# x in two layouts, s_dst as a row sent by DMA, norms scaled on either engine, and issue by due time, in a four-layer graph kernel

## The chip, the cores and the metric

One core of one Trainium2 chip. The metric is the device time of one execution in microseconds (us). Every kernel here was timed in several rounds beside the kernel before on the same chip, and its result compared with the reference. A program can fall into a slower state. Where a kernel is named, "after" is the changed kernel.

## The reference, cut to what matters

64 graphs of 256 nodes with 128 features share one adjacency matrix. Four layers follow each other, each closed by a layer norm of (x + layer(x)) without weights. The kernel treats two graphs at a time (a "pair"; 32 pairs).

```python
# layer 0, five steps
    m_in = jnp.einsum('nm,bmd->bnd', in_matrix, h)         # av = [m_in, m_out]; both matrices are adj
    z = jax.nn.sigmoid(av @ w3_w.T + w3_b + u3)             # u3 = h @ u3_w.T + u3_b
    r = jax.nn.sigmoid(av @ w4_w.T + w4_b + u3)
    hv = jnp.tanh(av @ w5_w.T + w5_b + (r * h @ u5_w.T + u5_b))
    h = (1.0 - z) * h + z * hv
# layer 1: a product with fixed softmax weights (cut)
# layer 2, attention
    h = jnp.einsum('bmi,ih->bmh', x, Wp) + bp
    s_src = jnp.einsum('bmh,h->bm', h, a_src)
    s_dst = jnp.einsum('bmh,h->bm', h, a_dst)
    scores = s_src[:, :, None] + s_dst[:, None, :]          # leaky relu, mask, softmax, times A
    h_gat = jax.nn.relu(_layernorm(jnp.einsum('bmn,bnh->bmh', weighted_adj, h), gat_g, gat_b))
    # then an aggregation, two products with a norm between them, relu(... + h_gat) (cut)
# layer 3: polynomials of adj, each with its weight (cut)
x = _layernorm(x + layer(x))                                # after every layer
```

There are six norms per pair, 192 in all: four between layers, one after the attention, one inside layer 2.

## The kernel before: the parts that the change touches

The kernel describes its work as operations with tiles read and written, an engine and a duration. A small list scheduler of its own (`Schedule`) orders them, and they are then emitted to the tile framework in that order. The parts that matter:

```python
# Schedule.order: the next operation is the one with the least key
key = (start + (us if len(op.ways) > 1 else 0.0), min(op.pair, self.n_pairs - ABREAST), -op.rest, op.number)
...
# every norm: statistics on VectorE, the root on GpSimd
def stats(y, eps=None):
    ...
    pool(1.04, lambda: nc.gpsimd.tensor_tensor(rs(), rs(), neg_half.ap, op=ALU.pow), [s, neg_half], [s])   # L422
    return s, mv, rs
# five of six norms: scaled on VectorE, (x - mean) * rs, straight from the root
def layer_norm(y, o):
    s, mv, rs = stats(y)
    ... nc.vector.tensor_scalar(tokens(o)[:, c, :], tokens(y)[:, c, :], mv()[:, c, 0:1], rs()[:, c:c + 1],
                                op0=ALU.subtract, op1=ALU.mult)                                          # L430
def layer0(x0):
    hT = to_sbuf(transposes(x0, tokens), "hT")            # x turned by TensorE
    ...
def layer2(x2):
    ...
    # s_dst, already repeated on all partitions, by one product of 512 columns
    pe(mm(512), lambda: nc.tensor.matmul(sd.at(512), vdst.ap, xT.at(512), start=True, stop=True), [vdst, xT], [sd])
    ...
    # the attention norm only: -mean * rs on VectorE (L549), then four activations on ScalarE (L553)
# emission, at the end
for op, fn in S.order(tiles):
    for v, ap in op.tiles.items():
        v.ap = ap
    fn()
```

## Time and profile before

| | before |
|---|---|
| time, median of 3 | 1832.8 us (1831.24 to 1833.34) |
| TensorE (PE) busy | 1741.1 us, 95% |
| PE idle, 50 to 1600 us | 36 us |
| PE idle, from 1600 us on | 49 us |
| VectorE (DVE) / ScalarE (ACT) busy | 1194.5 / 793.5 us |
| GpSimd (POOL) busy | 438.8 us |

Read it as: an engine that is almost always busy, with a short tail where it is not. The idle times are lengths of a stretch less PE's busy time in it; the prediction shows the lines.

### The profile page before, as it was taken

Reading aid. Unit: us, or ns where it says so; the run is one execution under the profiler, and the core shown is the slowest. Engines: PE = TensorE matmul, PEld = TensorE weight load, DVE = VectorE, ACT = ScalarE, POOL = GpSimd, SP = SyncE. Lnnn points to the kernel's source line nnn. Section 1 sums busy time; section 2 is a strip of 40 time slices with the busy share of each in tenths; the row PEclk is TensorE's granted clock in tenths of the full one; section 3 lists DMA queues with packets and bytes.
Section 4 is the critical chain, followed back from the end, with each engine's and each line's share of the span. In section 5 each row is a group of like instructions: output and inputs, shape, how many; then the busy total and the mean of one; then the engine's idle time right before and its main releaser. Section 6 shows DMA issues by size and latency. Waiting matters only on the chain. (4 is left out here: it accounts for less than half of the span.)

```text
span 1832.3 us, 22228 instructions
## 1 busy us (share of the span) xinstructions
PE 1741.1 (95%) x7856; PEld 1230.3 (67%) x7856; DVE 1194.5 (65%) x3536; ACT 793.5 (43%) x1586; POOL 438.8 (24%) x519
## 2 busy tenths in 40 slices
PE   8999999999999999999999999999999999998767
PEld 6567576767767667676776666666766667665566
DVE  5466666667767667667776577665667666665753
ACT  3444445444445454434444444444444444443322
POOL 0022212312231221222222212231123222111152
PEclk9999999999999999999999999999999999999778
DMA  4000000000000000000000000000000000000000
GB/s 119 1 1 12 12 12 1 12 12 13 7 12 7 18 6 7 12 13 11 8 13 12 13 12 1 12 12 7 7 0 7 6 7 7 6 1 6 1 1 24
DMA packets 35024, 20.50 MB, mean 11 GB/s; under 512 B 1248, under 2 KB 34528, under 8 KB 34912
## 3 DMA queue, kind: packets, MB, share of 16 engines
q1 hardware_dynamic: 34912, 19.08, 3.6%
q8 instruction: 61, 1.00, 0.2%
q14 instruction: 51, 0.42, 0.1%
HBM read 10.69 MB, written 8.39 MB: 10 GB/s over the span
## 5 line engine op out<-in xcount | busy, mean ns | idle before, releaser
L173 ACT COPY a<-ps 128x512 f32<-128x512 f32 (+1 forms) x532 | 278.5, 541 | 483.5 <-PE ps L400 286.0
L419 POOL TENSOR_SCALAR s<-s 128x4 f32<-128x4 f32 x160 | 49.5, 310 | 986.1 <-DVE s L416 986.1
L400 PE MATMUL ps<-aT,a 128*128 128x256 f32 x1024 | 242.8, 379 | 1.7 <-ACT a L173 1.6
L400 PEld LDWEIGHTS ps<-aT,a 128*128 128x128 f32 x1024 | 189.9, 190 | 49.5 <-issue 24.5
L422 POOL TENSOR_TENSOR s<-s,neg_half 128x4 f32<-128x4 f32 x192 | 200.4, 1044 | 15.9
L430 DVE TENSOR_SCALAR x<-a,s 128x128 f32<-128x128 f32 x384 | 120.9, 370 | 100.1 <-POOL s L422 99.9
L462 DVE TENSOR_TENSOR a<-a,a 128x512 f32<-128x512 f32 x160 | 121.0, 756 | 95.4 <-ACT a L460 95.2
L460 ACT ACTIVATE a<-ps,bzrh 128x512 f32<-128x512 f32 x160 | 109.9, 687 | 160.6 <-PE ps L458 160.5
L446 ACT ACTIVATE a<-ps,bzrh 128x512 f32<-128x512 f32 x160 | 109.4, 685 | 160.1 <-PE ps L443 156.8
L448 DVE SCALAR_TENSOR_TENSOR a<-a,a 128x512 f32<-128x512 f32 x160 | 120.9, 759 | 81.1 <-ACT a L446 80.5
L414 DVE BATCH_NORM_STATS2 s<-a 128x6 f32<-128x128 f32 x640 | 141.5, 279 | 47.9 <-ACT a L173 45.7
L450 PE MATMUL ps<-a,w 128*128 128x512 f32 x320 | 163.0, 600 | 7.2 <-ACT a L446 7.0
L458 PE MATMUL ps<-a,u5h 128*128 128x512 f32 x320 | 164.4, 595 | 4.9 <-DVE a L448 4.9
L443 PE MATMUL ps<-a,w 128*128 128x512 f32 x320 | 163.6, 593 | 1.8 <-ACT a L173 1.8
L457 PE MATMUL ps<-a,w 128*128 128x512 f32 x320 | 164.5, 596 | 0.0
L442 PE MATMUL ps<-a,W 128*128 128x512 f32 x320 | 163.9, 594 | 0.0
L481 PEld LDWEIGHTS ps<-W,a 128*128 128x128 f32 x1024 | 131.7, 196 | 36.6 <-issue 17.9
L481 PE MATMUL ps<-W,a 128*128 128x128 f32 x1024 | 135.6, 281 | 8.7 <-DVE a L488 4.4
L452 ACT ACTIVATE a<-ps,bzrh 128x512 f32<-128x512 f32 x160 | 110.0, 688 | 62.7 <-PE ps L450 61.3
L400 PE MATMUL ps<-aT,x 128*128 128x256 f32 x512 | 129.3, 391 | 8.1 <-DVE x L430 7.7
L463 DVE SCALAR_TENSOR_TENSOR a<-a,a 128x512 f32<-128x512 f32 x160 | 118.5, 745 | 16.3 <-ACT a L452 13.9
L382 PEld LDWEIGHTS ps<-ident,a 128*128 128x128 f32 x768 | 92.4, 142 | 53.3 <-issue 23.2
(140 smaller groups left out, 2645.6 us busy)
## 6 DMA issues: line engine op xcount, KB each, us to landing
x<-x_in SPq DMA_DIRECT2D x32, 256.0 KB, 2.8
y_out<-a SPq DMA_DIRECT2D x32, 256.0 KB, 2.3
W<-mats_in SPq DMA_DIRECT2D x1, 832.0 KB, 6.7
W<-mats_in SPq DMA_DIRECT2D x1, 512.0 KB, 3.7
rbc<-rows_in SPq DMA_DIRECT2D x1, 385.0 KB, 7.2
aT<-adjT_in SPq DMA_DIRECT2D x1, 256.0 KB, 4.7
a<-adj_in SPq DMA_DIRECT2D x1, 256.0 KB, 5.9
ccol<-cols_in SPq DMA_DIRECT2D x1, 6.0 KB, 3.5
```

The source lines that it names most:

```text
L173: S.add([("ACT", us_act, lambda: nc.scalar.copy(o(), i())), ("DVE", us_dve, lambda: nc.vector.tensor_copy(o(), i()))], r, w)
L400: nc.tensor.matmul(t.at(2, N)[:, b, :], tokens(i)[:, 2 * b + j, :], right.ap[:, j, :], start=(j == 0), stop=(j == 1))
L414: nc.vector.bn_stats(st.at(4, 6)[:, c, :], tokens(y)[:, c, :])
L422: pool(1.04, lambda: nc.gpsimd.tensor_tensor(rs(), rs(), neg_half.ap, op=ALU.pow), [s, neg_half], [s])
L430: nc.vector.tensor_scalar(tokens(o)[:, c, :], tokens(y)[:, c, :], mv()[:, c, 0:1], rs()[:, c:c + 1], op0=ALU.subtract, op1=ALU.mult)
L442: nc.tensor.matmul(t.at(512), mat("u3"), hT.at(512), start=True, stop=False)
L443: nc.tensor.matmul(t.at(512), w345.ap[:, 1, :], mT.at(512), start=False, stop=True)
L450: pe(mm(512), lambda t=t, mT=mT: nc.tensor.matmul(t.at(512), w345.ap[:, 0, :], mT.at(512), start=False, stop=True, skip_group_check=True), ...
L457: nc.tensor.matmul(t.at(512), w345.ap[:, 2, :], mT.at(512), start=True, stop=False)
L458: nc.tensor.matmul(t.at(512), u5h.ap, r.at(512), start=False, stop=True)
L462: dve(0.7, lambda hv=hv, hT=hT: nc.vector.tensor_sub(hv.at(512), hv.at(512), hT.at(512)), [hv, hT], [hv])
L481: nc.tensor.matmul(tokens(t)[:, c, :], i.at(4, P)[:, c, :], w(), start=(k == 0), stop=(k == len(lefts) - 1))
```

## The change

Its intent: take work off TensorE (the first transposes of layer 0, because x is also loaded turned; the s_dst product, because s_dst comes as a column of a product that is made anyway, is turned on VectorE and goes over DRAM to all partitions), let the scheduler choose ScalarE or VectorE for the scaling of each norm, and order the operations so that the last pairs do not march in step. The core of the diff (set-up of weights, tuned durations and renamings cut):

```diff
-                    key = (start + (us if len(op.ways) > 1 else 0.0), min(op.pair, self.n_pairs - ABREAST), -op.rest, op.number)
+                    key = (start + (us if len(op.ways) > 1 else 0.0), self.due(op.pair) - op.rest, op.number)
...
+DUE, LAST_DUE, LAST = 50.0, 10.0, 7
+    def due(self, pair):
+        late = max(pair - (self.n_pairs - LAST), 0)
+        return DUE * (pair - late) + LAST_DUE * late
...
     def load_x(p):
+        load(lambda: hTs[p].at(2, N), xT[2 * p:2 * p + 2].rearrange("b d n -> d b n"), hTs[p])
...
-    def layer0(x0):
-        hT = to_sbuf(transposes(x0, tokens), "hT")
+    def layer0(x0, hT):
...
+        nmr = lambda: s.at(32)[:, 12:16]
+        dve(0.16, lambda: nc.vector.scalar_tensor_tensor(nmr(), mv()[:, :, 0], -1.0, rs(), op0=ALU.mult, op1=ALU.mult), [s], [s])
+        return s, rs, nmr
+
+    def normalize(y, o, s, rs, nmr):
+        ...
+        S.add([("ACT", 1.85, by_act), ("DVE", 1.45, by_dve)], [y, s], [o])
...
-        pe(mm(512), lambda: nc.tensor.matmul(sd.at(512), vdst.ap, xT.at(512), start=True, stop=True), [vdst, xT], [sd])
+        dve(0.34, lambda: nc.vector.transpose(srow.at(4, 32), hs()[:, :, D - 30:D + 2]), [h], [srow])
+        S.add([("SP", 0.45, lambda: nc.sync.dma_start(line([32, 4], [P, 4], [1, 32]), srow.at(4, 32)[31::32]))], [srow], [d], 3.2)
+        S.add([("SP", 0.45, lambda: nc.sync.dma_start(sd.at(512), line([0, P], [1, 512])))], [d], [sd], 5.5)
```

## The prediction

> **What bounds the kernel now.** I read four views of the profile, in this order. First the page's engine totals and its forty slices.
>
> ```profile
> span 1832.3 us, 22228 instructions
> ...
> PE 1741.1 (95%) x7856; PEld 1230.3 (67%) x7856; DVE 1194.5 (65%) x3536; ACT 793.5 (43%) x1586; POOL 438.8 (24%) x519
> ...
> PE   8999999999999999999999999999999999998767
> ...
> PEclk9999999999999999999999999999999999999778
> DMA  4000000000000000000000000000000000000000
> ```
>
> TensorE is busy 95% of the span, VectorE 65%, ScalarE 43%, the DMA engines almost never. The last three slices are different: TensorE falls to 0.7 to 0.8 busy, and its granted clock falls with it. So there are two regimes, and the second view, busy time by stretch (columns: stretch, length, busy time of PE, PEld, DVE, ACT, POOL, granted clock, DMA share, GB/s), measures them:
>
> ```profile
> 0.00:6.10 6.10, 0.00 (x0) 0.00 (x0) 1.99 (x14) 1.28 (x1) 0.83 (x7) 1.00 0.71 209
> ...
> 50.00:1650.00 1600.00, 1563.83 (x7047) 1094.49 (x7047) 1064.98 (x3082) 720.12 (x1427) 385.76 (x446) 1.00 0.03 9
> 1650.00:1832.30 182.30, 133.60 (x644) 106.31 (x642) 102.35 (x379) 56.17 (x130) 52.16 (x66) 0.84 0.03 8
> ```
>
> From 50 to 1650 us TensorE idles 36 us in 1600, at full clock. After 1650 it idles 49 us in 182 and runs at 0.84. The third view, the chain that ended last (start, length, what), shows why:
>
> ```profile
> 1656.41 6.91 PE ps L400 x32
> ...
> 1690.63 8.65 PE ps L400 x32
> ...
> 1757.60 1.22 POOL a L557
> 1758.82 1.23 POOL a L556
> ...
> 1789.96 10.18 PE ps L400 x32
> 1800.13 1.75 PE ps L382 x16
> ```
>
> One spread of one pair is 8 records (4 matmuls in two passes each), so x32 is four pairs doing the same stage one after the other: the last four pairs, which have equal priority, march in step. All four want TensorE together, then VectorE together, then GpSimd together. The same 32 records take 6.91 us at 1656 and 10.18 us at 1790: that is the lowered clock. The fourth view, groups by form, prices what the change removes:
>
> ```profile
> L382 PE MATMUL ps<-ident,x 128*128 128x128 f32 x512 | 77.5, 279 | 2.9 <-DVE x L430 2.9
> L505 PE MATMUL ps<-wpx,a 128*128 128x129 f32 x256 | 35.0, 277 | 0.0
> L510 PE MATMUL ps<-a,vdst 128*128 128x512 f32 x64 | 34.2, 616 | 0.0
> ```
>
> L382 on x is four sets of 4 transposes per pair, one of which goes; L510 is the s_dst product, which goes whole. The mean of one record overlaps its neighbours; the chain gives the true spacing: four transposes in 0.44 us, one 512-column product in 0.86 us, one spread in 1.73 us.
>
> **What the Trainium skill says.** (1) "TensorE: Matmul & The Clock Gate", Part 1: the clock is throttled unless the engine has been busy lately. The trace agrees: 1.00 where it idles 2%, 0.84 where it idles 27%. So an idle gap in the tail costs twice. (2) "Trace Analysis", Optimization Strategy: where the bound engine changes over time, interleaving the regimes may help. This tail is such a place: from 1700 to 1750 us DVE is busy 36.15 of 50 us and PE 35.67. (3) "VectorE: DVE Perf Modes", The three transpose paths: the VectorE transpose turns 32x32 blocks only. That is why s_dst comes out as four rows, one per block, and needs a DMA to be joined; no trace here has this operation yet. (4) "DMA: Bandwidth & Descriptors", Anatomy of one DMA: some 2.0 us fixed per transfer, and waits are taken by the issuing sequencer. The trace agrees: y_out lands 2.3 us after issue, x 2.8 us.
>
> **The change, part by part.** *x loaded in both layouts.* Removes the first transposes of layer 0: 32 x 0.44 = 14.1 us of TensorE, and 32 evacuations of 0.59 us, mostly on ScalarE. Adds 32 transfers of 256 KB, which are small beside a DMA share of 0.03. At the start, xT and x of pair 0 both stand ahead of adjT in the queue, so the first spread (6.9 us now) comes perhaps 0.8 us later; a product on xT can start ahead of it.
>
> *s_dst by block turn and DMA.* Removes 32 x 0.86 = 27.5 us of TensorE and one PSUM bank for that time. Adds one column to 128 products (35.0/129 = 0.3 us), 32 turns on DVE (estimate 0.3 us each, from the 128x128 forms at 0.28) and two DMAs in series: estimated 0.4 + 2.3 + 0.4 + 2.8 = 5.9 us against 0.86 us of product. This is in the chain of one pair but not of the core: the order keeps several pairs open at once, and the new schedule reserves more (0.45 + 3.2 + 0.45 + 5.5).
>
> *Norm scaling on ACT or DVE.* In the built order 101 of the 192 norms are on DVE and 91 on ACT (before: 160 and 32). The busy time of one scaling is (120.9 + 76.0)/640 = 0.31 us on DVE (the two L430 groups) and 49.5/128 = 0.39 us on ACT (L553). DVE loses 59 x 4 x 0.31 = 73 us and gains 160 x 0.16 = 26 us of the small -mean*rstd product and 10 us of turns: 1194 - 73 + 36 = 1157, give or take 30. ACT gains 59 x 4 x 0.39 = 92 and loses 24 copies of 0.59, 14: about 871 us, half of the span. Neither becomes the bound.
>
> *Issue by due time.* Moves nothing in amount, but the order changes throughout. I summed the TensorE work in the order in which the instructions stand, with the spacings above. Before, the last four pairs have 52, 51, 49 and 47 us of TensorE work left at their attention product, and 6.1, 4.3, 2.6 and 0.9 us at their last product: in step. After, the last seven have 133, 121, 109, 89, 86, 54 and 40 us left there, and 69.6, 55.7, 41.3, 28.2, 16.0, 8.2 and 0.9 at the end: a staircase, so while one pair normalizes another multiplies.
>
> **The sum, by stage.** The before kernel: the 639 records left at 1650 us are 112 us of work at the spacings above, and over the first 1650 us busy time was 1.5% above such a sum (1607.5 against 1584), so 113 us at full clock; they took 133.6 busy us. Slow clock thus cost 20 us. 1832 = 1721 (work) + 6 (start) + 36 (steady idle) + 49 (tail idle) + 20 (slow clock).
>
> After: work 1721 - 14.1 - 27.5 + 0.3 = 1679, since on an engine that is 98% busy removed work counts in full. Start 7. Steady idle 26: the waits there are short ones on DVE and ACT (longest 2.5 us), the planned durations are closer to the measured ones and a PSUM bank is freed; I take a quarter off. Tail idle: the last pair still has a chain after its attention product. Adding row durations (three norms at 1.75 + 1.3 + 0.2 + 1.5, GpSimd's 2.6, layer 2's and 3's products, copies, some 30 hops at 0.2, the last DMA) gives about 49 us, beside which 40 us of TensorE work stands; so at least 9 us, plus imperfect filling over the last 110 us, where those late layers ask about as much of DVE as of PE: 18. Slow clock 7, in proportion to that idle time. Sum: 1679 + 7 + 26 + 18 + 7 = 1737 us, 5.2% below.
>
> **Rivals.** *The staircase does not help:* late layers alone are limited by DVE and latency whatever their order, so tail and steady losses stay: 1679 + 7 + 36 + 49 + 20 = 1791 us, just over 2% faster. For it: DVE's 36 of 50 us at 1700. Against: layer 0 of late pairs now lies among them, and DVE is relieved. *The DMA detour becomes a wait:* the queue and DVE are both in order, so an add that waits for its row holds up every pair behind it. If half of the 32 held TensorE 2 us, 32 us come back: about 1769. Against it: the 9.6 us reserved for an estimated 5.9. *The steady state improves more than I allow:* least-slack order, fewer PSUM banks wanted and free choice of norm engine may cut 36 us of idle to 12: 1723. *ScalarE becomes the wait:* its copies release TensorE, and four extra 0.465 us activations (their spacing at L553) ahead of one delay it by 1.9 us; 91 times, mostly hidden; perhaps 10 us: 1747.
>
> **Range and chances.** The removed work alone is 41 us, 2.3%; only a new wait can undo it. The tail is worth between 0 and 55 us, the steady state between -30 and +24. So 1705 to 1768, and faster by over 2% at 0.95.
>
> **What would show it.** PE busy near 1686 us with the s_dst product gone; 96% or more of the span; a clock in the last three slices of 0.9 or more; in the chain no PE run of four pairs of one stage at the end; DVE near 1157 and ACT near 871 us; the row and its broadcast landing within 2 to 3.5 us each. If PE waits on the score add or the prelu behind it show tens of us, the detour rival is right; if the last 150 us still show PE at 70%, the staircase rival is. The prediction is wrong above 1768 or below 1705.

## More of the kernel before

One more view of this kernel is needed later, VectorE's waits (what waited, for what: us in total, times, longest):

```profile
DVE x L430 <- POOL s L422: 99.9, 76, 4.6
...
DVE a L430 <- POOL s L422: 69.2, 59, 3.2
...
DVE s L549 <- POOL s L422: 35.5, 29, 1.4
```

VectorE stands 205 us at work that follows GpSimd's root (L422). TensorE idles only 36 us in the middle all the same.

In the kernel after, the root is L434, the small product -mean * rs L436 (now of all 192 norms, and between root and scaling), the scaling L442 on VectorE and L447 on ScalarE.

## The result, and the profile after

| | median us | range | runs |
|---|---|---|---|
| before (same rounds) | 1832.0 | 1831.12 to 1833.34 | 4 |
| after | 1831.6 | 1828.94 to 1833.58 | 4 |

The ratio is 0.9996, with a 95% interval of 0.9979 to 1.0014: no change that the runs can tell from none, where 5.2% less was predicted. The result is correct.

The page of the kernel after, its totals and slices (TensorE's busy tenths, then its granted clock):

```profile
span 1831.8 us, 22230 instructions
...
PE 1707.2 (93%) x7664; PEld 1197.9 (65%) x7664; DVE 1158.6 (63%) x3479; ACT 870.2 (48%) x1802; POOL 442.8 (24%) x519
...
PE   8999999999999899999998999999899999998886
...
PEclk9999999999999999999999999999999999999999
```

The work went as intended: 192 PE records fewer (128 transposes, 32 products in two passes each), VectorE and ScalarE where the prediction has them. The end improved: the clock stays at nine tenths or more in each of the last slices. But 8s now stand in the middle of the PE row. Busy time by stretch of the kernel after (stretch, length, then PE, PEld, DVE, ACT, POOL, clock, DMA share, GB/s):

```profile
50.00:1600.00 1550.00, 1472.70 (x6513) 1017.96 (x6512) 983.26 (x2855) 739.02 (x1498) 358.96 (x411) 0.99 0.06 17
...
50.00:1650.00 1600.00, 1520.12 (x6723) 1050.11 (x6722) 1014.39 (x2948) 764.13 (x1555) 368.06 (x422) 0.99 0.06 17
1650.00:1831.80 181.80, 142.83 (x788) 120.00 (x786) 116.18 (x455) 88.47 (x220) 73.95 (x91) 0.92 0.06 17
```

and the same first stretch of the kernel before:

```profile
50.00:1600.00 1550.00, 1514.23 (x6857) 1063.98 (x6857) 1033.04 (x3007) 695.27 (x1380) 377.53 (x437) 1.00 0.03 9
```

In the same 1550 us TensorE ran 6513 records where it ran 6857. With 7664/32 = 239.5 records per pair against 245.5 that is the work of 27.2 pairs against 27.9: the steady state became slower, although each pair asks less of TensorE. Its idle time there went from 36 to 77 us. The gain of the removed work was given back in the middle. Who holds TensorE up? The waits of the kernel after, VectorE's first, then ScalarE's, then TensorE's:

```profile
DVE s L436 <- POOL s L434: 206.7, 178, 4.6
...
DVE b L536 <- DMA a<-d: 27.2, 16, 5.8
...
ACT a L574 <- POOL a L573: 80.8, 25, 4.6
...
PE ps L390 <- DVE a L484: 29.2, 18, 4.3
PE ps L469 <- ACT a L465: 18.0, 16, 3.2
```

TensorE waits for layer 0's update (L484) on VectorE, an engine that is busy only 63% of the time. One such place, VectorE's timeline (start, length, line, operation; in brackets how long the engine was idle before it and whom it waited for):

```profile
636.48 0.66 DVE L481 TENSOR_TENSOR a<-a,a 128x512 f32<-128x512 f32 x1
638.38 0.16 DVE L436 SCALAR_TENSOR_TENSOR s<-s 128x4 f32<-128x4 f32 x1 [1.24 <-POOL s L434]
638.46 0.69 DVE L482 SCALAR_TENSOR_TENSOR a<-a,a 128x512 f32<-128x512 f32 x1
639.07 0.34 DVE L442 TENSOR_SCALAR x<-a,s 128x128 f32<-128x128 f32 x1
639.32 0.69 DVE L484 SCALAR_TENSOR_TENSOR a<-a,a 128x512 f32<-128x512 f32 x1
```

GpSimd's and TensorE's timelines at the same place:

```profile
637.31 1.04 POOL L434 TENSOR_TENSOR s<-s,neg_half 128x4 f32<-128x4 f32 x1
```

```profile
636.40 1.02 PE L462 MATMUL ps<-a,w 128*128 128x512 f32 x2
640.15 1.08 PE L390 MATMUL ps<-ident,a 128*128 128x128 f32 x4 [2.73 <-DVE a L484]
```

L481, L482 and L484 are one chain of layer 0, on whose end TensorE waits. In VectorE's queue the tiny product of another pair's norm (L436, 0.16 us) stands between them, ahead of its time: its root is still under way on GpSimd until 638.35. VectorE stands for 1.24 us, and TensorE stands 2.73 us. (The programs can be rebuilt, and VectorE's instructions in this trace are in the order of the rebuilt program, line by line. In the kernel's own list L482 has place 2016, L484 place 2020, the product place 2026 and its first scaling, L442 at 639.07, place 2038: both were put ahead.) The Trainium skill says in "TensorE: Matmul & The Clock Gate", section "Architectural detail: the array is 16× 32×32, not 1× 128×128", that ScalarE and VectorE are strict FIFO; this trace agrees, since L482 did not pass the product that waited.

The idle is not all of the price. The four transposes at 640.15 show 1.08 us, where four take 0.44 in the chain of this kernel (`1578.19 0.44 PE ps L390 x4`). The granted clock (third figure from the end) tells most of it:

```profile
639.50:642.80 3.30, 2.65 (x9) 2.32 (x10) 3.30 (x7) 0.59 (x1) 0.00 (x0) 0.50 0.00 0
642.90:646.00 3.10, 3.10 (x19) 2.79 (x18) 0.29 (x2) 0.98 (x2) 0.00 (x0) 1.00 0.26 85
```

At the end of this gap the clock was halved for 3.4 us, so the work that came after it also took more busy time. Not every gap is: of the twelve over 2 us in the middle, three had a stretch at half clock at their end. In all the trace has eleven such stretches, 54 us, five of them in the middle, and TensorE was busy for 40 us of them.

Is that the order that the kernel's scheduler made? I matched the operations in the traces with each kernel's own list (some nine in ten can be matched), and counted those that an operation listed later had overtaken on its engine:

| overtaken operations | before | after |
|---|---|---|
| TensorE | 0.7% | 1.5% |
| VectorE | 32% | 57% |
| ScalarE | 12% | 46% |

The tile framework, which takes the emitted instructions, puts them in another order; by what rule, no run here shows. (The rebuilt programs, counted by instruction and with none left unmatched, say the same: TensorE 1.7% and 2.7%, VectorE 41% and 58%, ScalarE 13% and 40%. The percentages in the expectations below are partly counts of that kind.) TensorE, whose order I had looked at, keeps the list; the two engines that feed it do not. That was the theory to test.

### The profile page after: what moved, and what is told of

Read it like the earlier page. It is cut to its first block, busy times and chain, and to the rows that moved or that the text cites. A ratio compares the mean times of both kernels' runs of the same rounds, so it can differ in the third digit from the quotient of the medians.

```text
span 1831.8 us, 22230 instructions
## 1 busy us (share of the span) xinstructions
PE 1707.2 (93%) x7664; PEld 1197.9 (65%) x7664; DVE 1158.6 (63%) x3479; ACT 870.2 (48%) x1802; POOL 442.8 (24%) x519
## 5 line engine op out<-in xcount | busy, mean ns | idle before, releaser
L180 ACT COPY a<-ps 128x512 f32<-128x512 f32 (+1 forms) x508 | 267.4, 537 | 346.9 <-PE ps L412 210.3
L412 PE MATMUL ps<-aT,a 128*128 128x256 f32 x1024 | 250.0, 384 | 6.9 <-ACT a L180 6.5
L434 POOL TENSOR_TENSOR s<-s,neg_half 128x4 f32<-128x4 f32 x192 | 204.7, 1066 | 15.8
L469 PE MATMUL ps<-a,w 128*128 128x512 f32 x320 | 165.5, 605 | 18.0 <-ACT a L465 18.0
L436 DVE SCALAR_TENSOR_TENSOR s<-s 128x4 f32<-128x4 f32 x192 | 40.7, 212 | 207.0 <-POOL s L434 206.7
L462 PE MATMUL ps<-a,w 128*128 128x512 f32 x320 | 164.9, 597 | 5.7 <-ACT a L180 5.7
L476 PE MATMUL ps<-a,w 128*128 128x512 f32 x320 | 165.7, 600 | 0.0
L481 DVE TENSOR_TENSOR a<-a,a 128x512 f32<-128x512 f32 x128 | 93.2, 728 | 103.1 <-ACT a L479 102.8
L500 PEld LDWEIGHTS ps<-W,a 128*128 128x128 f32 x1024 | 127.4, 192 | 41.5 <-issue 12.4
L390 PEld LDWEIGHTS ps<-ident,a 128*128 128x128 f32 x768 | 93.0, 142 | 83.3 <-DVE a L484 37.8
L390 PE MATMUL ps<-ident,a 128*128 128x128 f32 x768 | 115.6, 276 | 29.4 <-DVE a L484 29.2
L467 DVE SCALAR_TENSOR_TENSOR a<-a,a 128x512 f32<-128x512 f32 x128 | 93.0, 728 | 75.9 <-ACT a L465 75.5
L461 PE MATMUL ps<-a,W 128*128 128x512 f32 x256 | 131.2, 594 | 0.0
```

The lines of the kernel that those rows point to most:

```text
L180: S.add([("ACT", us_act, lambda: nc.scalar.copy(o(), i())), ("DVE", us_dve, lambda: nc.vector.tensor_copy(o(), i()))], r, w)
L390: nc.tensor.transpose(t.at(4, P)[:, c, :], x_like(i)[:, c, :], ident.ap)
L412: nc.tensor.matmul(t.at(2, N)[:, b, :], tokens(i)[:, 2 * b + j, :], right.ap[:, j, :], start=(j == 0), stop=(j == 1))
L461: nc.tensor.matmul(t.at(512), mat("u3"), hT.at(512), start=True, stop=False)
L462: nc.tensor.matmul(t.at(512), w345.ap[:, 1, :], mT.at(512), start=False, stop=True)
L469: pe(mm(512), lambda t=t, mT=mT: nc.tensor.matmul(t.at(512), w345.ap[:, 0, :], mT.at(512), start=False, stop=True, skip_group_check=True), ...
```

## The experiments

**Theory:** the plan's order, not its amounts, is lost on the way to the chip; VectorE (and ScalarE) then stand behind results of GpSimd. **Rivals:** the DMA detour is the new wait; ScalarE's additional norm scalings are; the due times do not pay.

### 1. The order held, and the due times alone

The framework leaves an instruction behind another if it is told of a dependency. *after_pinned* and *before_pinned* tie every instruction to the one emitted before it on its engine, without a semaphore:

```diff
+    newest = {}
     for op, fn in S.order(tiles):
         ...
+        done = len(nc.cur_bb.bb.instructions)
         fn()
+        for i in nc.cur_bb.bb.instructions[done:]:
+            if i.engine in newest:
+                tc.add_manual_dep(i, newest[i.engine].name, mybir.DependencyInfo(
+                    mybir.DependencyClass.NoSync, mybir.DependencyReason.DATA), reason="plan order")
+            newest[i.engine] = i
```

*after_old_rank* puts only the old key back into the kernel after; *before_due* puts only the new key and `due` into the kernel before. Neither is held.

> The changed kernel with every instruction held behind the previous one of its engine in the kernel's own plan, so that the framework beneath it can no longer re-sort them. Theory A (re-sorting: in the changed kernel's trace the four scalings of one norm stand apart, with other groups' work between them, and 46% of ScalarE's and 57% of VectorE's operations were overtaken by one planned later, against 12% and 32% before): the plan comes through, 1740 to 1770 us, PE idle in the middle back to 40 us or less. Theory B (the DMA detour of s_dst or the moved norms cost the time themselves): within 1% of 1832. Theory C (least slack with 50 us per pair is a worse order than lowest pair first): within 1% of 1832 or slower.

> The kernel before with the same pinning. Theory A: little was re-sorted there, so 1800 to 1835 us, a gain of under 2%. If re-sorting is harmless or useful everywhere (B, C): 1832 or slower.

> The changed kernel with the old rank of operations (lowest pair first, last four equal) instead of due times; everything else of the change stays. Theory C: faster than 1832 by at least 20 us. Theory A: which rank is used matters less than that it is kept; the saved 41 us of TensorE show only in part, 1800 to 1835. Theory B: about 1832.

> The kernel before with only the rank by due time. Theory C: slower than before by 20 us or more in the middle, less in the tail. Theory A: re-sorting grows with this rank, so about the same, 1820 to 1860, with more operations overtaken than before. Theory B: a better tail and nothing else, 1790 to 1815.

| | median us (range) | ratio to before [95%] |
|---|---|---|
| after_pinned | 1719.5 (1717.81 to 1720.89) | 0.9388 [0.9374, 0.9402] |
| before_pinned | 1783.4 (1782.94 to 1784.24) | 0.9739 [0.9723, 0.9756] |
| after_old_rank | 1865.9 (1864.92 to 1868.53) | 1.0190 [1.0175, 1.0206] |
| before_due | 1793.2 (1792.66 to 1795.73) | 0.9794 [0.9779, 0.9808] |

All correct. The count of overtaken operations in *after_pinned* is zero on every engine, and the same instructions in the planned order take 112 us less, more than was expected. The re-sorting costs the kernel before 49 us too, which was expected to be under 2%, so the plan's order was never what ran. Held against held, the change is worth 64 us, 3.6% (1783.4 to 1719.5). The page and the waits of *after_pinned*:

```profile
span 1716.9 us, 22198 instructions
...
PE 1675.2 (98%) x7664; PEld 1196.6 (70%) x7664; DVE 1176.7 (69%) x3479; ACT 882.5 (51%) x1802; POOL 449.9 (26%) x519
```

```profile
DVE s L436 <- POOL s L434: 58.1, 74, 2.2
...
ACT a L574 <- POOL a L573: 7.0, 11, 2.2
```

TensorE's idle time in the middle, which was 77 us, is 13:

```profile
50.00:1600.00 1550.00, 1536.68 (x6971) 1085.67 (x6970) 1069.95 (x3096) 803.25 (x1620) 400.03 (x450) 1.00 0.06 18
```

The wait at the small product falls from 207 to 58 us, the relu's (L574) from 81 to 7, and the wait for the DMA row (L536) is gone from the list. PE busy falls by 32 us for the same 7664 records. Some 13 us of that is the clock: TensorE was busy at half clock for 14 us here and for 40 us in the kernel after, and half of the difference is lost time. Most of the rest may be the end of the last record before each gap, which nothing overlaps (35 stretches of unbroken work here, 103 there, an estimated 0.16 us each, the 0.27 us of a transpose's record less the 0.11 us between two: 11 us); that part is an estimate. A stretch of VectorE's timeline shows the planned form, one small product and its four scalings together:

```profile
928.92 0.16 DVE L436 SCALAR_TENSOR_TENSOR s<-s 128x4 f32<-128x4 f32 x1 [0.20 <-POOL s L434]
929.00 1.11 DVE L442 TENSOR_SCALAR x<-a,s 128x128 f32<-128x128 f32 x4
```

The rival "due times do not pay" falls: alone they take 38 us off the kernel before, and taken out of the kernel after they cost 34. (Both differences are clear of zero, though not of 2%.) My theory foresaw neither: *before_due* lies where the detour's theory (B) had it, and *after_old_rank* is slower than any of the three allowed.

### 2. The two engines' queues held, and each part undone without holding

*after_pin_both* holds only ScalarE and VectorE (the condition above with `and str(i.engine).split('.')[-1] in ('Activation', 'DVE')`). The other three undo one part of the change each, with nothing held:

```diff
# after_old_norms: layer norms by VectorE from the mean, the attention norm by ScalarE
-        normalize(y, o, *stats(y))
+        s, mv, rs, _ = stats(y)
+        ... nc.vector.tensor_scalar(..., mv()[:, c, 0:1], rs()[:, c:c + 1], op0=ALU.subtract, op1=ALU.mult)
# after_no_detour: s_dst by the product again
+        pe(mm(512), lambda: nc.tensor.matmul(sd.at(512), vdst.ap, xT.at(512), start=True, stop=True), [vdst, xT], [sd])
# after_no_xT: x turned by TensorE again
-        layer0(xs[p], hTs[p])
+        layer0(xs[p], turn(xs[p], "hT"))
```

> The changed kernel with only ScalarE's and VectorE's instructions held in plan order; TensorE, GpSimd and the DMA queue stay free. If the loss comes from these two in-order engines being re-sorted (theory A, now in this narrower form), nearly the whole gain of pinning everything comes back: 1715 to 1735 us. If TensorE's or the DMA queue's few shifts did it: above 1780.

> The changed kernel, not pinned, with the norms scaled as before (five on VectorE from mean and rstd, the one of layer 2 on ScalarE). In the built order ScalarE's instructions overtaken fall from 40% to 22%, VectorE's from 58% to 52%. Theory A with the norms as the trigger (a scaling waits for GpSimd and is put ahead of work that does not): 1775 to 1805 us, ahead of the changed kernel by 1.5% or more. With the DMA detour as the trigger: 1820 to 1840.

> The changed kernel, not pinned, with s_dst by the 512-column product as before: 27.5 us more TensorE work. VectorE's instructions overtaken fall from 58% to 50%, ScalarE's from 40% to 35%. With the detour as the trigger of the re-sorting: 1800 us or less in spite of the added work. With the norms as the trigger: 1835 to 1860, the added work showing in part.

> The changed kernel, not pinned, with the first transposes of layer 0 back on TensorE instead of the second layout of x: 14.1 us more TensorE work and 32 more copies. Nothing about it should feed the re-sorting (VectorE 54%, ScalarE 35% overtaken), so every theory expects the added work in part: 1830 to 1850 us. Faster than 1825 would say that the loads or their three buffers cost time.

| | median us | ratio to before [95%] |
|---|---|---|
| after_pin_both | 1718.2 | 0.9379 [0.9365, 0.9393] |
| after_old_norms | 1780.0 | 0.9718 [0.9704, 0.9733] |
| after_no_detour | 1828.2 | 0.9976 [0.9959, 0.9993] |
| after_no_xT | 1820.5 | 0.9938 [0.9923, 0.9952] |

All correct. Holding ScalarE and VectorE is the whole of holding. In the re-sorted order, undoing the norms helps by 52 us, the x load by 11 and the detour by 3, which is within the noise, although the last two put work back on TensorE (PE busy 1729.2 us without the detour). No theory foresaw the last two: *after_no_detour* lies between its two ranges, and *after_no_xT* below its range, where its expectation blames the loads. Experiment 3 clears the loads. The detour's rival is thus half right: in this order the detour gives back what it saves. But without it the middle still idles 62 us (1550 less 1487.68), so it is not the cause.

### 3. GpSimd's root taken away, and each part undone in the planned order

*after_recip* is **wrong**: a reciprocal on VectorE stands for GpSimd's root, and the small add before it moves to VectorE too (cut below), so no norm passes GpSimd for its root; nothing is held. (A power on VectorE, which would have been right, did not compile.) The others are the undoings with every instruction held.

```diff
-        pool(1.04, lambda: nc.gpsimd.tensor_tensor(rs(), rs(), neg_half.ap, op=ALU.pow), [s, neg_half], [s])
+        dve(0.16, lambda: nc.vector.reciprocal(rs(), rs()), [s], [s])
```

> The changed kernel, not pinned, with the reciprocal root of the norms replaced by a plain reciprocal on VectorE, so that no scaling waits for GpSimd. Wrong result on purpose. The framework still re-sorts (VectorE 56%, ScalarE 31% overtaken). If the loss is the in-order engines standing at the head of a norm that GpSimd has not finished (DVE L436 waited 206.7 us for POOL L434, 58.1 when pinned): 1750 to 1780 us. If the shuffling of the other work is what costs, whatever it waits for: 1815 to 1840.

> Norms scaled as before, all else changed, every engine in plan order. Says what the free choice of engine is worth where the order is kept: if it helps the late layers as intended, 1730 to 1750 us against 1719.5; if it is worth nothing by itself, within 5 us of 1719.5.

> s_dst by the 512-column product as before, all else changed, every engine in plan order. By the prediction's sum the removed work counts in full where TensorE is 98% busy: 1719.5 + 27 = 1747 us, 1742 to 1752. If the detour costs waits of its own even in plan order, less than 1735.

> The old rank (lowest pair first, last four equal) with all else changed, every engine in plan order. By the prediction's sum the due times are worth the tail and a little: 1719.5 + 40 to 50 = 1760 to 1770 us. If the old rank was bad only through the re-sorting (1866 unpinned): within 15 us of 1719.5.

> First transposes of layer 0 on TensorE as before, all else changed, every engine in plan order. By the prediction's sum 14.1 us more TensorE work, in full: 1728 to 1738 us against 1719.5. If the second layout's loads or its three buffers cost something by themselves: below 1725.

| | median us | ratio to before [95%] |
|---|---|---|
| after_recip (wrong result) | 1720.0 | 0.9389 [0.9373, 0.9404] |
| after_old_norms_pinned | 1712.2 | 0.9346 [0.9332, 0.9359] |
| after_no_detour_pinned | 1739.8 | 0.9496 [0.9482, 0.9510] |
| after_old_rank_pinned | 1754.5 | 0.9579 [0.9565, 0.9593] |
| after_no_xT_pinned | 1731.1 | 0.9459 [0.9445, 0.9473] |

The four held ones are correct. Against *after_pinned* (1719.5) each part has its worth in the planned order: due times 35 us, detour 20, x load 12, and the free choice of norm engine minus 7. *after_old_norms_pinned*, the change without that choice, is the fastest correct version of all, 6.5% below the kernel before; its expectation allowed a loss or nothing, not this gain. The detour and the due times are each worth a little less than expected. The x load gains 12 us where the order is kept, so its loads cost nothing by themselves.

The reciprocal brings everything back without holding anything. Its page:

```profile
span 1718.2 us, 22158 instructions
...
PE 1676.8 (98%) x7664; PEld 1191.9 (69%) x7664; DVE 1203.8 (70%) x3871; ACT 869.2 (51%) x1794; POOL 176.4 (10%) x135
```

Its queues are still re-sorted, 55% of VectorE's and 35% of ScalarE's operations being overtaken. So re-sorting alone need not be slow; it is slow where it meets GpSimd's late roots. One reserve: the kernel's plan and the framework's order are both made anew with the shorter norm, so it is not the same order with the root taken out. Whether the shorter norm is itself the gain is answered in experiment 5, where both kernels are held. The gain is more than was expected (1750 to 1780 us).

### 4. Only the small product held, or all but it

The first three groups left open whether L436 alone carries the loss. Its 192 instructions are marked (`.nmr = True` on the operation), and the loop of experiment 1 acts on them alone (*after_hold_nmr*) or on all others (*after_free_nmr*):

```diff
+            if i.engine in newest and hasattr(op, "nmr"):                       # hold_nmr
+        for i in [] if hasattr(op, "nmr") else nc.cur_bb.bb.instructions[done:]:   # free_nmr
```

> Only the 192 small -mean*rstd products are held behind the VectorE instruction that precedes them in the plan; all else stays free to be re-sorted (VectorE 53%, ScalarE 37% overtaken). If the place of this product, the first follower of GpSimd in each norm, is the whole loss: 1715 to 1745 us. If other followers of GpSimd or the rest of the shuffling matter too: 1760 to 1810.

> The reverse: everything is held in plan order but these 192 products, which the framework may place (VectorE 17% overtaken, ScalarE none). If the product alone is the loss: 1790 us or more. If not: 1715 to 1745.

*after_hold_nmr* took 1761.5 us (ratio 0.9617 [0.9599, 0.9635]), *after_free_nmr* 1749.3 (0.9558 [0.9542, 0.9574]); both correct. Holding 192 small instructions brings back 70 of 112 us; freeing them alone loses 30. So they are a large piece, and not all; no other group was held alone. *after_free_nmr* lies just above the range for "not the product alone". The waits of *after_free_nmr* warn against a short cut:

```profile
DVE s L436 <- POOL s L434: 212.7, 186, 2.8
...
ACT a L575 <- POOL a L574: 8.6, 10, 2.2
```

VectorE waits 213 us for the root, as long as in the kernel after (207) and before (205), and loses only 30. The total of a wait does not measure the loss. That what stands behind it does is my reading; no run isolates it.

### 5. One queue held at a time

ScalarE's waits behind GpSimd had doubled (its relu, and its scalings, which wait for VectorE's small product and so for the root: 60.9 + 47.2 us before, 80.8 + 66.2 + 62.2 after), VectorE's had not. So I suspected ScalarE, and held one queue each (the condition of *after_pin_both* with one name). *after_recip_pinned* (wrong) holds everything without GpSimd's root.

> Only ScalarE's instructions are held in the plan's order; VectorE's queue stays re-sorted. Held on both, the time was 1718; held on neither, 1831.6. Theory A (what hurts is ScalarE standing behind results of GpSimd: those waits were 108 us before and 209 after, 11 when held, and follow the loss from kernel to kernel): most of the 112 us comes back, 1735 to 1765, and ScalarE's waits for the small product and for GpSimd's adds fall below 60 us. Theory B (what hurts is VectorE standing there; its wait for GpSimd's root is 207 us): little comes back, 1790 to 1825, and VectorE's wait stays at 190 us or more.

> Only VectorE's instructions are held in the plan's order; ScalarE's queue stays re-sorted. Theory B (VectorE's place in line is what hurts): most comes back, 1730 to 1760, VectorE's wait for GpSimd's root near 60 us. Theory A (ScalarE's): 1780 to 1815, with ScalarE's wait for GpSimd's add before its relu still at 70 us or more. If each alone brings back about half, both queues count alike.

> Wrong on purpose: the norm's root is a reciprocal on VectorE, and every instruction is held in the plan's order. The same kernel re-sorted took 1720. If re-sorting costs only through results of GpSimd, holding the order changes little here: 1705 to 1720. If re-sorting costs in itself, as much again should come off: 1650 to 1690, of which the work on TensorE (1675) allows at best some 1690.

| | median us (range) | ratio to before [95%] |
|---|---|---|
| after_pin_scalar | 1785.5 (1782.65 to 1787.62) | 0.9743 [0.9729, 0.9758] |
| after_pin_vector | 1737.6 (1737.51 to 1738.87) | 0.9484 [0.9470, 0.9498] |
| after_recip_pinned (wrong result) | 1714.6 (1714.31 to 1717.11) | 0.9362 [0.9346, 0.9377] |

My suspicion fell, although ScalarE's part is more than the other theory allowed. VectorE's order alone brings back 94 of 112 us, ScalarE's 46; they overlap. The middle of *after_pin_vector*, then its waits, VectorE's and ScalarE's:

```profile
50.00:1600.00 1550.00, 1532.65 (x6919) 1076.24 (x6918) 1052.85 (x3038) 785.05 (x1600) 395.35 (x442) 1.00 0.06 18
...
DVE s L436 <- POOL s L434: 58.2, 72, 2.1
...
ACT a L574 <- POOL a L573: 68.0, 29, 3.6
```

ScalarE's relu still waits 68 us there, at little cost. With ScalarE held instead, that wait is 9.4 us, but TensorE still waits for VectorE's update:

```profile
PE ps L390 <- DVE a L484: 26.0, 17, 3.4
```

And without GpSimd's root, holding is worth 5 us instead of 112 (1720.0 to 1714.6). With the order held, taking the root away is worth 5 us as well (1719.5 to 1714.6), so a shorter norm is not what *after_recip* gained by; the loss needs both, the other order and the root on GpSimd.

### The kernels side by side

PE's span split into busy and idle, from the windows of each profiled run (they sum to the span):

| us | PE busy | idle 0 to 50 | idle 50 to 1600 | idle from 1600 | span |
|---|---|---|---|---|---|
| before | 1741.1 | 6 | 36 | 49 | 1832.3 |
| before_pinned | 1719.3 | 6 | 2 | 54 | 1781.2 |
| after | 1707.2 | 6 | 77 | 42 | 1831.8 |
| after_pin_scalar | 1696.4 | 7 | 37 | 41 | 1780.9 |
| after_pin_vector | 1683.3 | 7 | 17 | 29 | 1735.8 |
| after_pinned | 1675.2 | 8 | 13 | 20 | 1716.9 |
| after_recip | 1676.8 | 5 | 18 | 19 | 1718.2 |

## Why the prediction was wrong, point by point

The prediction's sum, with its own windows (steady up to 1650 us, tail after it) and what the kernel after shows. Slow clock is half of the time in which TensorE was busy while the trace's clock record stood at one half (45.0 us before, 40.1 after, 14.3 held); work is PE's busy time less that.

| us | predicted | after |
|---|---|---|
| work | 1679 | 1687 |
| start | 7 | 6 |
| steady idle | 26 | 80 |
| tail idle | 18 | 39 |
| slow clock | 7 | 20 |
| sum | 1737 | 1832 |

**Removed work: right.** 192 records went, and in the planned order PE is busy 1675.2 us for a predicted 1686 (1679 of work and 7 of slow clock; the held kernel's slow clock is 7). In the order that ran it is 1707.2, 93% of the span where 96% was predicted.

**VectorE 1157 and ScalarE 871: right**, at 1158.6 and 870.2. **The turn at 0.3 us: right.** The group of the kernel after:

```profile
L532 DVE STREAM_TRANSPOSE a<-h 128x128 f32<-128x128 f32 x32 | 9.8, 307 | 0.4
```

**The detour at 5.9 us in series: near enough**, 5.1 us from the turn to the add in the chain of the kernel after. The row lands after 1.61 us, a little under the 2 to 3.5 predicted, and the broadcast after 3.19:

```profile
1582.21 0.23 DVE a L532
...
1582.46 1.61 DMA d<-a
...
1584.13 3.19 DMA a<-d
...
1587.35 0.69 DVE b L536
```

**Tail idle 18, slow clock 7 and a clock of 0.9: the mechanism right, the size only in the planned order.** From 1600 us on, idle falls from 54 to 20 us between the two held kernels, and from 49 to 42 between those that were predicted. The clock rises from 0.84 to 0.92 in the last 182 us, but half-clock stretches now come in the middle, so the slow clock took 20 us and not 7. No run of four pairs in step stands in the chain's end any more.

**"Steady idle 26": this step failed.** The prediction reads: "the waits there are short ones on DVE and ACT (longest 2.5 us), the planned durations are closer to the measured ones and a PSUM bank is freed; I take a quarter off". It took the kernel's plan for the order on the chip. Measured: 77 us of idle (50 to 1600 us; 80 to 1650) instead of fewer than 36, and 32 us more of PE busy time than the same records take when held. TensorE does keep the plan, which is where the staircase was read. VectorE and ScalarE do not, and I never compared their order with the plan or with who produces their inputs. Every input of the sum that depends on planned waits (steady idle, tail idle, the reserve of 9.6 us for the detour) hung on that.

**What the change made worse.** The cost of re-sorting, each kernel against itself held, is 49 us before, 68 for *after_old_norms*, 88 for *after_no_detour*, 89 for *after_no_xT*, 112 after and 111 with the old rank. So the norms' new form, the detour and the x load each add to it, and overlap; the norms add most (112 less 68), and the due times add nothing. What they do is shown: without GpSimd's root re-sorting costs 5 us, and VectorE's queue carries most of it. Why the framework places followers of GpSimd so early is not shown. It may take GpSimd's results as ready sooner than they are; no run here looks into it. Nor is it settled why the same 205 us of VectorE's wait cost the kernel before so much less. A count in the rebuilt programs fits the reading that it is what stands behind: in the kernel after, 353 of VectorE's 404 scaling instructions stand ahead of work that the plan puts before them, and 119 of the 192 small products; in the kernel before it is 261 of 640. That is no test of it.

**The rivals.** "The staircase does not help": wrong, the due times are worth 35 us held and 34 not held. "The DMA detour becomes a wait": its size, about 32 us back, is what the re-sorted order shows (3 us faster with 27.5 us more product work), but held it gains 20 of the 27.5 predicted, and the wait for its row vanishes when VectorE's order is held. "ScalarE becomes the wait", perhaps 10 us: the free choice of engine cost 7 in the planned order; whether through ScalarE's copies is not shown. "The steady state improves more": held, 13 us of idle where that rival had 12, and 1719.5 us in all where it had 1723; but a held kernel was not what was predicted, so this agreement is no merit of the prediction. A worse steady state is in none of the four, except as the detour's wait. The range does not follow from its own extremes, either: 1791 us (the removed work alone) with nothing from the tail and 30 us lost in the steady state is 1821, not 1768.

## What to carry to other kernels

If a kernel plans its own order, compare the built order with the plan on every engine, not on the busiest one alone, before arguing from the plan; and if they differ, hold the plan's order and measure. In an in-order queue, a tiny instruction placed ahead of its producer can cost what stands behind it: look for small instructions with a wait ahead of the chain that the bound engine needs, and do not judge by the total of the wait. Work removed from the bound engine counts only while that engine stays fed: here 41 us of it, together with the other parts, bought nothing in the order that ran, and the change is worth 64 us once both kernels are held.

## What the Trainium skill lacked or had wrong

- "Perfetto Trace Analysis", section "Optimization Strategy": it gives too few buffers as what repeated gaps on the busy engine can mean. Here they came, with the same buffers, from the order in a feeding engine's queue: holding VectorE's order alone took TensorE's idle in the middle from 77 to 17 us and the time from 1831.6 to 1737.6.
- "GPSIMD Engine Reference", section 3.1 "Elementwise — side-by-side cycle accounting", times an add of 2048 elements, and has no figure for a power or for tiny tiles. Here the power on 128x4 took 1037 ns and an add of a constant on the same tile 229 ns, where VectorE's reciprocal on it took 177 ns (medians).
- "VectorE: DVE Perf Modes", section "The three transpose paths": 311 ns for 128x128 in bf16. The same shape in f32 took 307 ns here (mean of 32), so about the same for four-byte elements, for which the section gives no figure.
